# A recurrent kernel's matmuls regrouped: output rows by half of batch and column set, 256 columns an instruction

## The chip, the cores and the metric

The kernel runs on one core of a Trainium2 chip. A core has a matrix engine (TensorE, in the profile PE for its matmuls and PEld for its weight loads), VectorE (DVE), ScalarE (ACT), GpSimd (POOL) and SyncE (SP), whose queue issues most DMAs. SBUF is the working memory of 128 partitions; PSUM, of 8 banks, takes the results of matmuls. The metric is the device time of one execution in microseconds.

## The reference

A GRU over 128 time steps, whose outputs are added to its input. Batch 64, width 512; all in float32.

```
do_prop = ((t + 1) % 4 == 0) & (t < T - 1)
z = sigmoid([x_t, h] @ Wz + bz)
r = sigmoid([x_t, h] @ Wr + br)
c = tanh([x_t, r * h] @ Wh + bh)
h_new = (1 - z) * h + z * c              # the output of step t
h     = tanh(h_new @ Wp + bp) if do_prop else h_new
out[:, t] = x[:, t] + h_new
```

Each of Wz, Wr and Wh is 1024 x 512: the upper half multiplies x_t, which is known for all steps ahead, and the lower half multiplies h, which is not. So a step has three dependent-on-h products (R and Z from h, H from r * h), a fourth (P, with Wp) every fourth step, and products of x that may be done at any time before.

## The kernel before

**Layout.** The 64 batch rows are two halves of V = 32. A tensor such as h, z or the output has partitions 32q to 32q + 31 for column quarter q (J = 128 columns) and, along the free axis, half h and then the 128 columns: tile [128, 2, 128]. VectorE's 32x32 block transpose (`turn`, L223) makes of it hT, whose slices of 32 columns are the stationary operands, with 128 partitions of contraction.

**Matmuls.** `products` (L195) issues four matmuls, one for each quarter q. All have the same 32-column stationary operand; each streams its own quarter of the weights, 128 columns (96 in the x products), and writes PSUM partitions 32q to 32q + 31. `gate` (L206) calls it for two halves, half 0 first through all four contraction pieces, then half 1: 32 matmuls for a gate. A float32 matmul of the code is two recorded matmuls, each with its weight load: the profile shows 64 for a gate.

**The products of x** are formed for four or eight steps together by a scheme of seven products in place of eight, applied twice: `batch` (L438) covers two of the outer seven products, with seven inner products j each into four scratch banks (q, r, a, x). A *unit* (L442) is one inner product of one outer one: 8 matmuls of the code, 16 recorded, of 96 columns. A batch of two has 14 units. When a batch's first four inner products are done, `end_1` reads them out (ScalarE copies of the x and q banks, two VectorE additions), and after all seven `end_2` does (one copy, three additions). GpSimd then adds batches and biases into tiles cp (L509 to L557), and makes the sums of x that the units need as stationary operands (s12r, s34r, s4r, o, s; L289 to L327). `plain` and `plain_last` (L396, L409) do the first and last steps directly with 128-column matmuls.

**Order.** Each engine's program is in the order of the code. A step (L598 on) is: gate R; for each half sigmoid (ScalarE), r * h (VectorE), transpose; `seed`, which copies the x part of the next step's gate from cp into the gate's PSUM bank, so that the next gate's matmuls accumulate onto it; gate Z; two activations over 256 columns, sigmoid of z and sigmoid of -z, and keep = (1 - z) h; places[0] units; gate H; for each half tanh, times z, plus keep, transpose; places[1] units; in every fourth step gate P, tanh and transpose for each half, places[2] units; then GpSimd's work of that step. The numbers of units are in PLACES (L560), by u, the place in a round of eight steps, and in HEAD and TAIL for the first and last steps. `fill` (L372) runs units from a queue and defers their read-outs to `pending`; `read_out` (L379) issues them behind the next gate. A round of eight steps takes 98 units. u = 0 and 4 are the steps with gate P.

**PSUM.** Four banks for gates: r0 (half 0 of R and of P), r1 (half 1 of R, of P and of H), h (half 0 of H), z (Z, both halves); four scratch banks. The activations of R and H write their result in place into PSUM.

The 112 matmuls of zeros at the start (L185) keep TensorE busy while weights load.

Of the kernel before, what the change touches and what calls it, by code (L numbers as in the profile page):

```python
# [12 lines left out]
AF = mybir.ActivationFunctionType  # L13
PSUM = bass.MemoryType.PSUM
# [3 lines left out]
def kernel(  # L18
# [17 lines left out]
    P = 128  # L36
# [11 lines left out]
    assert V * NQ == P and D == H and J == P and T % 8 == 0  # L48

# [54 lines left out]
    bias_in = const.tile([P, 4, J], F32, name="bias")  # L104
# [37 lines left out]
    for q in range(NQ):  # L142
        nc.sync.dma_start(
            out=bias_in[part(q), 3, :],
            in_=bp[ts(q, J)].rearrange("(o n) -> o n", o=1).broadcast_to([V, J]),
        )

    rec = [ps_c.tile([P, 4, J], F32, name=f"rec_{n}") for n in ("r0", "r1", "h", "z")]  # L150
    zz = rec[3][:, :S]
    P_ = 3

    def half(i, h):
        if i == Z:
            return zz[:, h]
        if i == H_:
            return (rec[2][:, 0], rec[1][:, 2])[h]
        return rec[h][:, 0 if i == R else 1]

    scratch = [ps_c.tile([P, 4 * J], F32, name=f"scratch_{n}") for n in "qrax"]
    q_ps, r_ps, a_ps, x_ps = (
# [3 lines left out]
    bias = bias_in.rearrange("p i (c n) -> p c i n", c=C)  # L166

    def spread(bank, rows, which):
        bank = bank.rearrange("p (i n) -> p i n", i=4)
        n = len(which)  # L170
        for q in range(NQ):
            nc.tensor.matmul(
                bank[part(q), 0:n, :],
                lhsT=ones,
                rhs=bias_row[:, rows, ts(q, J)],
                start=True,
                stop=True,
            )
        for j, i in enumerate(which):
            nc.scalar.copy(bias_in[:, i, :], bank[:, j, :])  # L180

    bias0 = bias[:, 0, 0:3, :]
    bias_d = const.tile([P, 3, J // 2], F32, name="bias_d")

    def idle(n):  # L185
        for i in range(n):
            nc.tensor.matmul(
                rec[i // NQ % 4].rearrange("p c n -> p (c n)")[part(i % NQ)],
                lhsT=zeros[:, :V],
                rhs=zeros,  # L190
                start=True,
                stop=True,
            )

    def products(ps, lhs, rhs, start=False):  # L195
        for q in range(NQ):
            nc.tensor.matmul(  # L197
                ps[part(q)],
                lhsT=lhs,
                rhs=rhs(q),  # L200
                start=start,
                stop=True,
                skip_group_check=True,
            )

    def gate(i, lT, w):  # L206
        for h in range(S):
            for k in range(K):
                products(
                    half(i, h), lT[:, h, ts(k, V)], lambda q: w[:, k, ts(q, J)]  # L210
                )

    def product(ps, lT, w, k, start=False):
        c0, s0 = divmod(k, C)
        for h in range(S):
            products(
                ps[:, ts(h, J)],
                lT[:, c0, s0 * B + h * V : s0 * B + (h + 1) * V],
                lambda q: w[:, k, ts(q, J)],
                start and h == 0,  # L220
            )
# [137 lines left out]
    def seed(i, t):  # L359
        if t >= T:  # L360
            return
        src = G[t][:, :, :, i, :].rearrange("p c h n -> p h c n")
        if i == Z:
            nc.scalar.copy(zz.rearrange("p h (c n) -> p h c n", c=C), src)
            return
        for h in range(S):
            nc.scalar.copy(half(i, h).rearrange("p (c n) -> p c n", c=C), src[:, h])  # L367

    queue = []
    pending = []  # L370

    def fill(n):  # L372
        for _ in range(min(n, len(queue))):
            unit, end = queue.pop(0)
            unit()
            if end is not None:
                pending.append(end)

    def read_out():  # L379
        while pending:  # L380
            pending.pop(0)()

    def banks(t):
        first, second = scratch[:2] if t % 2 == 0 else scratch[2:]
        return (first[:, : S * J], first[:, S * J :], second[:, : S * J])

    def add_bias(t, gates):
        new_cp(t // 2)
        for i in gates:
            nc.vector.tensor_add(  # L390
                G[t][:, :, :, i, :],
                banks(t)[i].rearrange("p (h c n) -> p c h n", h=S, c=C),
                bias[:, :, i, :].unsqueeze(2).to_broadcast([P, C, S, J // 2]),
            )
# [43 lines left out]
    def batch(n, ms):  # L438
# [3 lines left out]
        def unit(ps, m, j, e, start):  # L442
            g, i = ms[m]
            a, b = terms(i)[e]
            left, right = lhs(g, a, j), factor(b, j)
            for h in range(S):
                products(
                    ps[:, m, h].rearrange("p (g u) -> p g u", g=3),
                    left[:, ts(h, V)],
                    lambda q: right[:, q],  # L450
                    start and m == 0 and e == 0 and h == 0,
                )
# [11 lines left out]
        def blocks(b, a):  # L464
            return MB[n][:, :nm, b].rearrange("p m h g (a u) -> p m a (h g) u", a=2)[:, :, a]
# [6 lines left out]
        def end_1():  # L472
            MB[n] = mbp.tile([P, 2, 2, S, 3, J // 2], F32, tag="mb", name=f"mb_{what}")
            for m, (g, i) in enumerate(ms):
                M[g, i] = MB[n][:, m]
            T2[n] = copied("cx", "cx", x_ps)
            q1 = copied("cq", "cq", q_ps)
            nc.vector.tensor_add(T2[n][:, :nm], r_ps[:, :nm], T2[n][:, :nm])  # L478
            nc.vector.tensor_add(blocks(0, 0), runs(a_ps[:, :nm]), runs(q1[:, :nm]))

        def end_2():
            q2 = copied("cq", "cq2", q_ps)
            nc.vector.tensor_add(blocks(0, 1), runs(r_ps[:, :nm]), runs(q2[:, :nm]))  # L483
            nc.vector.tensor_add(blocks(1, 0), runs(x_ps[:, :nm]), runs(q2[:, :nm]))
            nc.vector.tensor_add(blocks(1, 1), runs(q_ps[:, :nm]), runs(T2[n][:, :nm]))  # L485

        free = units(a_ps, 2, True)
        one_ = [units(r_ps, 5, True), units(x_ps, 7, True), units(q_ps, 1, True)]

        one_ = sum(one_[2:] + one_[:2] if n in ((1, 0), (1, 1)) else one_, [])  # L490
        two_ = units(x_ps, 4, False) + units(q_ps, 6, False) + units(r_ps, 3, False)
        seq = [(u, None) for u in free + one_ + two_]
        size = sum(len(terms(i)) for _, i in ms)
        for n_units, end in ((4 * size, end_1), (7 * size, end_2)):
            seq[n_units - 1] = (seq[n_units - 1][0], end)
# [19 lines left out]
    def with_bias(g, i, v):  # L515
        m = M[g, i].rearrange("p b h g u -> p (b h) g u")
        nc.gpsimd.tensor_add(m, m, v.unsqueeze(1).to_broadcast([P, 4, 3, J // 2]))  # L517
# [37 lines left out]
    def pair_right(a, p1, x_, g=1):  # L555
        with_bias(g, x_, bias[:, 1, 0:3, :])
        add(c_block(g, a, 1), m_(g, p1), m_(g, x_))  # L557
# [3 lines left out]
        (8, 3, 0), (3, 8, 0), (6, 8, 0), (6, 8, 0), (6, 4, 0), (4, 6, 0), (8, 6, 0), (8, 6, 0),  # L561
    )
    HEAD = {0: (12, 12, 0), 1: (8, 6, 0), 2: (16, 12, 0), 3: (8, 6, 8), 4: (6, 8, 0)}
# [13 lines left out]
    for e in range(3):  # L577
# [4 lines left out]
        if e == H_:  # L582
            read_out()
            for i in range(3):
                seed(i, 0)
        fill(4)
        if e == R:
            spread(scratch[3], slice(0, 2), (R, H_))
            spread(scratch[1], slice(2, 3), (Z,))
            nc.gpsimd.tensor_sub(bias_d, bias[:, 1, 0:3, :], bias0)  # L590
# [3 lines left out]
    read_out()  # L594
# [3 lines left out]
    for t in range(T):  # L598
# [44 lines left out]
        read_out()  # L643
# [14 lines left out]
        rhT = new_T("rhT", f"rhT_{t}")  # L658
        for s_ in range(S):
            r = half(R, s_)  # L660
            nc.scalar.activation(r, r, AF.Sigmoid)  # L661
            nc.vector.tensor_mul(rh[:, s_, :], r, h[:, s_, :])  # L662
# [10 lines left out]
        nc.scalar.activation(z, zz, AF.Sigmoid)  # L673
        nc.scalar.activation(zz, zz, AF.Sigmoid, scale=-1.0)  # L674
        nc.vector.tensor_mul(keep, zz, h)  # L675
# [6 lines left out]
        if prop:  # L682
            for s_ in range(S):
                nc.scalar.copy(half(P_, s_), bias_in[:, 3, :])
        if last:
            nc.gpsimd.tensor_add(xr[g][:, j], xr[g][:, j], keep)
# [13 lines left out]
        read_out()  # L700
        h_new = two.tile([P, S, J], F32, tag="h", name=f"h_{t}")
        hT = None if last else new_T("hT", f"hT_{t}")
        for s_ in range(S):
            c = half(H_, s_)
            nc.scalar.activation(c, c, AF.Tanh)
# [9 lines left out]
            nc.vector.tensor_add(h_new[:, s_, :], c, keep[:, s_, :])  # L715
            turn(hT[:, s_, :], h_new[:, s_, :])
# [8 lines left out]
        if prop:  # L725
            gate(P_, hT, wp)
            read_out()
            h = two.tile([P, S, J], F32, tag="hprop", name=f"hprop_{t}")
            hT = new_T("hT", f"hpT_{t}")
            for s_ in range(S):  # L730
                nc.scalar.activation(h[:, s_, :], half(P_, s_), AF.Tanh)
# [113 lines left out]
```

## Time and profile before

Three runs took 1570.71, 1574.39 and 1577.15 us; the median is 1574.39. The profiled execution took 1573.8 us, its span is 1572.0 us.

| | busy us | share of the span | instructions |
|---|---|---|---|
| TensorE matmuls (PE) | 1369.3 | 87% | 51,920 |
| TensorE weight loads (PEld) | 1261.9 | 80% | 51,920 |
| VectorE (DVE) | 776.7 | 49% | 2,163 |
| ScalarE (ACT) | 561.7 | 36% | 1,858 |
| GpSimd (POOL) | 885.4 | 56% | 1,030 |

The granted clock of TensorE has a mean of 0.986: about three quarters in the first 78 us, 1.00 after that. The span has three parts: the first 78.3 us, in which weights load and step 0 runs; 127 steps of which eight in the middle take 94.5 us (from one GpSimd addition of a round, at 795.49 us, to the same in the next, at 890.03); and 4.8 us from the last matmul (1567.2 us) to the end, in which the last output is written.

How to read it: an idle time stands before an instruction with what ended it, an engine or a DMA; "issue" stands where nothing that the profile shows ended it. Matmuls overlap, so the mean duration of one (273 ns at 128 columns) isn't the distance to the next; rates are read from stretches.

### The profile page before, as it was taken

The numbers are of one execution on the slowest core, as the hardware profiler recorded it, in microseconds if no ns is written. First come the engines' busy times: TensorE is split into PE (matmuls) and PEld (weight loads), VectorE is DVE, ScalarE is ACT, GpSimd is POOL, SyncE is SP. The second block draws the span as 40 slices with busy tenths as digits, with TensorE's granted clock in tenths as the row PEclk, the third lists the DMA queues.
The fourth block names the chain that finished last, engine by engine and source line by source line (L and its number), as shares of the span: only waits on it lengthen the run. The fifth ranks groups of instructions, "written<-read, shape, count | busy, mean of one in ns | idle before, by whom it ended". The sixth has DMA issues, their size and how long they took to land.

```text
span 1572.0 us, 111797 instructions
## 1 busy us (share of the span) xinstructions
PE 1369.3 (87%) x51920; PEld 1261.9 (80%) x51920; DVE 776.7 (49%) x2163; ACT 561.7 (36%) x1858; POOL 885.4 (56%) x1030
## 2 busy tenths in 40 slices
PE   6588888889888888988888888889888988988888
PEld 4578888888788888888888888888778888878887
DVE  0345554554554554554554554554454555555544
ACT  0023333333333333333333333333333433333333
POOL 2276666656565665666656565565656655566520
PEclk7799999999999999999999999999999999999999
DMA  2321110111111111210111111111110111110021
GB/s 99 108 60 44 42 35 21 41 45 45 31 36 39 32 45 31 56 34 20 43 44 45 31 36 39 34 44 32 51 34 22 45 44 45 31 32 25 25 75 47
DMA packets 114221, 66.38 MB, mean 42 GB/s; under 512 B 12604, under 2 KB 108988, under 8 KB 113756
## 3 DMA queue, kind: packets, MB, share of 16 engines
q1 hardware_dynamic: 113048, 58.90, 13.5%
q8 instruction: 407, 6.67, 1.8%
q14 instruction: 58, 0.48, 0.1%
q10 hardware_dynamic: 452, 0.20, 0.0%
q0 software_dynamic: 256, 0.14, 0.0%
HBM read 42.41 MB, written 16.78 MB: 38 GB/s over the span
## 4 chain that ended last, share of the span: by engine, by line
PE 83%; issue 11%; SPq 3%; DMA 2%; POOL 1%; ACT 0%; DVE 0%; POOLq 0%; DVEq 0%; ACTq 0%
PE rec_r L197 27%; PE rec_z L197 15%; PE scratch_x L197 10%; PE scratch_q L197 10%; PE scratch_r L197 10%; PE rec_h L197 7%; PE scratch_a L197 5%; SPq L93 3%; DMA wh<-in_L_cond_Wh_dram 1%; DMA wh<-in_L_cond_Wr_dram 1%; DMA xr<-in_x_dram 0%; POOL cp L513 0%; POOL mb L517 0%; DVE keep L675 0%; ACT z L673 0%
## 5 line engine op out<-in xcount | busy, mean ns | idle before, releaser
L197 PE MATMUL rec_r<-wh,hT 128*32 128x128 f32 x6144 | 206.7, 273 | 32.4 <-issue 31.8
L197 PE MATMUL rec_z<-wh,hT 128*32 128x128 f32 x6144 | 207.7, 273 | 11.5 <-issue 9.9
L197 PEld LDWEIGHTS rec_r<-wh,hT 128*32 128x32 f32 x6144 | 176.7, 110 | 44.3 <-issue 43.2
L197 PEld LDWEIGHTS rec_z<-wh,hT 128*32 128x32 f32 x6144 | 180.3, 110 | 22.7 <-issue 22.1
L782 POOL TENSOR_TENSOR xr<-xr,h 128x256 f32<-128x256 f32 x127 | 92.8, 731 | 168.3 <-DVE h L715 159.6
L513 POOL TENSOR_TENSOR mb<-mb,mb 128x768 f32<-128x768 f32 x58 | 105.9, 1826 | 138.8 <-DVE mb L485 138.8
L197 PE MATMUL rec_h<-wh,rhT 128*32 128x128 f32 x4096 | 156.0, 273 | 21.8 <-issue 18.5
L197 PE MATMUL rec_r<-wh,rhT 128*32 128x128 f32 x4096 | 157.4, 273 | 15.7 <-issue 12.7
L513 POOL TENSOR_TENSOR cp<-mb,mb 128x768 f32<-128x768 f32 x75 | 136.9, 1826 | 48.0 <-DVE mb L485 36.5
L661 ACT ACTIVATE rec_r<-rec_r 128x128 f32<-128x128 f32 x256 | 67.1, 262 | 248.9 <-PE rec_r L197 248.9
L197 PEld LDWEIGHTS rec_h<-wh,rhT 128*32 128x32 f32 x4096 | 123.5, 110 | 31.5 <-issue 26.3
L197 PEld LDWEIGHTS rec_r<-wh,rhT 128*32 128x32 f32 x4096 | 127.0, 110 | 24.0 <-issue 20.1
L367 ACT COPY rec_r<-cp 128x128 f32<-128x128 f32 x384 | 102.7, 268 | 103.7 <-DVE h L715 68.9
L478 DVE TENSOR_TENSOR cx<-scratch_r,cx 128x384 f32<-128x384 f32 (+1 forms) x107 | 59.3, 554 | 158.3 <-ACT cx L469 158.3
L517 POOL TENSOR_TENSOR mb<-mb,bias 128x768 f32<-128x768 f32 x35 | 63.8, 1823 | 128.9 <-DVE mb L485 128.9
L469 ACT COPY cq<-scratch_q 128x384 f32<-128x384 f32 (+1 forms) x214 | 101.5, 474 | 66.0 <-PE scratch_q L197 63.6
L483 DVE TENSOR_TENSOR mb<-scratch_r,cq 128x384 f32<-128x384 f32 (+1 forms) x107 | 59.3, 554 | 119.5 <-PE scratch_r L197 96.0
L675 DVE TENSOR_TENSOR keep<-rec_z,h 128x256 f32<-128x256 f32 x96 | 40.8, 425 | 151.5 <-ACT rec_z L674 151.5
L673 ACT ACTIVATE z<-rec_z 128x256 f32<-128x256 f32 x128 | 49.1, 383 | 139.2 <-PE rec_z L197 139.2
L513 POOL TENSOR_TENSOR cp<-cp,mb 128x768 f32<-128x768 f32 x29 | 52.9, 1823 | 71.6 <-DVE mb L485 70.5
L662 DVE TENSOR_TENSOR rh<-rec_r,h 128x128 f32<-128x128 f32 x192 | 55.6, 290 | 64.5 <-ACT rec_r L661 63.9
L513 POOL TENSOR_TENSOR cp<-mb 128x768 f32<-128x768 f32 x47 | 85.7, 1824 | 2.7 <-ACT rec_r L367 0.2
(150 smaller groups left out, 3320.8 us busy)
## 6 DMA issues: line engine op xcount, KB each, us to landing
out_dram<-xr SPq DMA_DIRECT2D x249, 64.0 KB
xr<-in_x_dram SPq DMA_DIRECT2D x248, 64.0 KB
xs<-in_x_dram SPq DMA_DIRECT2D x240, 64.0 KB
wx<-in_L_cond_Wr_dram SPq DMA_DIRECT2D x7, 256.0 KB
wx<-in_L_cond_Wz_dram SPq DMA_DIRECT2D x7, 256.0 KB
wx<-in_L_cond_Wh_dram SPq DMA_DIRECT2D x7, 256.0 KB
wh<-in_L_cond_Wr_dram SPq DMA_DIRECT2D x4, 256.0 KB
wh<-in_L_cond_Wz_dram SPq DMA_DIRECT2D x4, 256.0 KB
```

The lines of the kernel that those rows point to most:

```text
L93: eng.dma_start(out=wt[:, k, :], in_=w.rearrange("(q k e) n -> k q e n", q=NQ, k=K)[k],)
L197: nc.tensor.matmul(ps[part(q)], lhsT=lhs, rhs=rhs(q), start=start, stop=True, skip_group_check=True,)
L367: nc.scalar.copy(half(i, h).rearrange("p (c n) -> p c n", c=C), src[:, h])
L469: nc.scalar.copy(c[:, :nm], ps[:, :nm])
L478: nc.vector.tensor_add(T2[n][:, :nm], r_ps[:, :nm], T2[n][:, :nm])
L483: nc.vector.tensor_add(blocks(0, 1), runs(r_ps[:, :nm]), runs(q2[:, :nm]))
L513: nc.gpsimd.tensor_add(dst, a, b)
L517: nc.gpsimd.tensor_add(m, m, v.unsqueeze(1).to_broadcast([P, 4, 3, J // 2]))
L661: nc.scalar.activation(r, r, AF.Sigmoid)
L662: nc.vector.tensor_mul(rh[:, s_, :], r, h[:, s_, :])
L673: nc.scalar.activation(z, zz, AF.Sigmoid)
L782: nc.gpsimd.tensor_add(xr[g][:, j], xr[g][:, j], h_new)
```

## The change

- `products` issues its four matmuls for half h of the batch and column set c: PSUM partitions 32(2h + c) on, with the stationary operand of half h, streaming two quarters of the weights, q = c and q = 2 + c, in one matmul of 256 columns (192 in the x products). A gate is 16 matmuls of the code in place of 32, a unit 4 in place of 8. Both halves run through the contraction together.
- So a gate's PSUM rows are by (h, c), and its free axis by d (quarter q = 2d + c). The rest of the kernel keeps the layout by quarter. `crossed` moves between them: each sigmoid or tanh of a half is two instructions on 64 partitions, which read partitions 64h on and write partitions 64d on of an SBUF tile. R, Z, H and P have four activations each (before: 2, 2, 2 and 2).
- r and c are SBUF tiles; the sigmoid of -z is gone, and keep is (z - 1) h from one VectorE instruction, so that h_new = c - keep, done for both halves in one instruction and turned in one.
- `seed` is one copy of 256 columns for every gate; biases are held in the new row order (bias_x, bias_p).
- Gates take three PSUM banks (r with P, z, h), scratch takes five: the x bank has a second one, y, and batches alternate.
- A batch's read-out is split into five parts, each put in the queue where its bank is complete (`end_x`, `end_q`, `end_r`, `end_q2`, `end_r2`), and run at once, with no `pending`. All batches use one order of inner products: a, x, q, r, x, q, r.
- PLACES is new: the units stand elsewhere in the steps, with 98 in a round as before, and 5 of them behind gate P in u = 0 and 4. HEAD differs by two units in step 4.

```diff
+    bias_x = const.tile([P, C, S, 3, J // 2], F32, name="bias_x")
+    bias_p = const.tile([P, S, J], F32, name="bias_p")
...
-    rec = [ps_c.tile([P, 4, J], F32, name=f"rec_{n}") for n in ("r0", "r1", "h", "z")]
-    zz = rec[3][:, :S]
+    rec = [ps_c.tile([P, S, 2, J], F32, name=f"rec_{n}") for n in "rzh"]
     P_ = 3
+    def gate_ps(i):
+        return rec[0][:, 1] if i == P_ else rec[i][:, 0]
+
+    scratch = [ps_c.tile([P, 4 * J], F32, name=f"scratch_{n}") for n in "qraxy"]
...
+    def quarters(v):
+        return v.rearrange("p n (d c j) -> p c n d j", d=2, c=2)
...
     def products(ps, lhs, rhs, start=False):
-        for q in range(NQ):
-            nc.tensor.matmul(
-                ps[part(q)],
-                lhsT=lhs,
-                rhs=rhs(q),
+        for h in range(S):
+            for c in range(2):
+                nc.tensor.matmul(
+                    ps[part(2 * h + c)],
+                    lhsT=lhs(h),
+                    rhs=rhs(c),
...
+    def gate(i, lT, w):
+        for k in range(K):
+            products(
+                gate_ps(i), lambda h: lT[:, h, ts(k, V)], lambda c: quarters(w)[:, c, k]
             )
...
+    def crossed(dst, h, ps, func):
+        for d in range(2):
+            nc.scalar.activation(
+                dst[ts(d, 2 * V), h, :], ps[ts(h, 2 * V), d, :], func
             )
...
     def seed(i, t):
+        if t < T:
+            nc.scalar.copy(
+                gate_ps(i).rearrange("p d (c n) -> p d c n", c=C),
+                G[t][:, :, :, i, :].rearrange("p c d n -> p d c n"),
+            )
...
-            for h in range(S):
-                products(
-                    ps[:, m, h].rearrange("p (g u) -> p g u", g=3),
-                    left[:, ts(h, V)],
-                    lambda q: right[:, q],
-                    start and m == 0 and e == 0 and h == 0,
-                )
+            products(
+                ps[:, m].rearrange("p d (g u) -> p d g u", g=3),
+                lambda h: left[:, ts(h, V)],
+                lambda c: right[:, c::2],
+                start and m == 0 and e == 0,
+            )
...
+        x_ps = x_two[len(T2) % 2]
...
+        for ps, j, start, end in (
+            (a_ps, 2, True, None),
+            (x_ps, 7, True, end_x),
+            (q_ps, 1, True, end_q),
+            (r_ps, 5, True, end_r),
+            (x_ps, 4, False, None),
+            (q_ps, 6, False, end_q2),
+            (r_ps, 3, False, end_r2),
+        ):
...
     PLACES = (
-        (8, 3, 0), (3, 8, 0), (6, 8, 0), (6, 8, 0), (6, 4, 0), (4, 6, 0), (8, 6, 0), (8, 6, 0),
+        (1, 8, 5), (1, 9, 0), (4, 8, 0), (6, 8, 0), (1, 8, 5), (6, 8, 0), (0, 8, 0), (1, 11, 0),
     )
-    HEAD = {0: (12, 12, 0), 1: (8, 6, 0), 2: (16, 12, 0), 3: (8, 6, 8), 4: (6, 8, 0)}
+    HEAD = {0: (12, 12, 0), 1: (8, 6, 0), 2: (16, 12, 0), 3: (8, 6, 8), 4: (6, 10, 0)}
...
+        r = two.tile([P, S, J], F32, tag="r", name=f"r_{t}")
         for s_ in range(S):
-            r = half(R, s_)
-            nc.scalar.activation(r, r, AF.Sigmoid)
-            nc.vector.tensor_mul(rh[:, s_, :], r, h[:, s_, :])
+            crossed(r, s_, gate_ps(R), AF.Sigmoid)
+            nc.vector.tensor_mul(rh[:, s_, :], r[:, s_, :], h[:, s_, :])
             turn(rhT[:, s_, :], rh[:, s_, :])
...
-        nc.scalar.activation(z, zz, AF.Sigmoid)
-        nc.scalar.activation(zz, zz, AF.Sigmoid, scale=-1.0)
-        nc.vector.tensor_mul(keep, zz, h)
+        for s_ in range(S):
+            crossed(z, s_, gate_ps(Z), AF.Sigmoid)
+        nc.vector.scalar_tensor_tensor(
+            out=keep, in0=z, scalar=1.0, in1=h, op0=ALU.subtract, op1=ALU.mult
+        )
...
         for s_ in range(S):
-            c = half(H_, s_)
-            nc.scalar.activation(c, c, AF.Tanh)
+            c = cand[:, s_, :]
+            crossed(cand, s_, gate_ps(H_), AF.Tanh)
             nc.vector.tensor_mul(c, c, z[:, s_, :])
...
-            nc.vector.tensor_add(h_new[:, s_, :], c, keep[:, s_, :])
-            turn(hT[:, s_, :], h_new[:, s_, :])
+        if not last:
+            nc.vector.tensor_sub(h_new, cand, keep)
+            turn(hT, h_new)
```

## The prediction

> **What bounds the kernel now.** I read four views, in this order: the page, the waits of the weight loads, their timeline, and the chain that ended last.
>
> ```profile
> span 1572.0 us, 111797 instructions
> ...
> PE 1369.3 (87%) x51920; PEld 1261.9 (80%) x51920; DVE 776.7 (49%) x2163; ACT 561.7 (36%) x1858; POOL 885.4 (56%) x1030
> ...
> q8 instruction: 407, 6.67, 1.8%
> ...
> PE 83%; issue 11%; SPq 3%; DMA 2%; POOL 1%; ACT 0%; DVE 0%; POOLq 0%; DVEq 0%; ACTq 0%
> ```
>
> TensorE is the bound: no other engine has a share worth naming in the chain. But 11% of that chain is "issue", time in which TensorE waits for nothing that the profile shows. The waits of the weight loads say how much (columns: total us, times, longest us):
>
> ```profile
> PEld rec_r L197 <- issue: 76.3, 99, 1.7
> PEld scratch_q L197 <- issue: 37.8, 55, 1.4
> PEld scratch_r L197 <- issue: 34.9, 54, 1.2
> PEld scratch_x L197 <- issue: 34.0, 50, 1.3
> PEld rec_h L197 <- issue: 26.3, 30, 1.7
> PEld rec_z L197 <- issue: 23.6, 47, 1.0
> PEld scratch_a L197 <- issue: 14.9, 26, 1.0
> ```
>
> That is 247.8 us in 361 holes, spread over all tiles in the same way, so no tile's data is late. The timeline says when they come (start, us, what, and in brackets the idle time before it):
>
> ```profile
> 800.13 1.03 PEld L197 LDWEIGHTS rec_r<-wh,hT 128*32 128x32 f32 x39 [1.53 <-issue]
> ...
> 803.97 0.16 PEld L197 LDWEIGHTS scratch_x<-tt,o 128*32 128x32 f32 x8 [0.52 <-issue]
> ...
> 807.51 0.25 PEld L197 LDWEIGHTS rec_r<-wh,rhT 128*32 128x32 f32 x9 [0.60 <-issue]
> ...
> 811.02 0.22 PEld L197 LDWEIGHTS scratch_q<-wx,o 128*32 128x32 f32 x9 [0.83 <-issue]
> ...
> 814.63 0.25 PEld L197 LDWEIGHTS rec_z<-wh,hT 128*32 128x32 f32 x10 [0.24 <-issue]
> ...
> 818.59 0.25 PEld L197 LDWEIGHTS rec_h<-wh,rhT 128*32 128x32 f32 x9 [1.16 <-issue]
> ...
> 822.36 0.23 PEld L197 LDWEIGHTS scratch_x<-tt,s12r 128*32 128x32 f32 x11 [0.84 <-issue]
> ...
> 825.87 1.13 PEld L197 LDWEIGHTS rec_z<-wh,hT 128*32 128x32 f32 x43 [0.34 <-issue]
> ```
>
> Work resumes after a hole every 3.68 us (25.74 us over 7). The page has 2 x 51920 TensorE instructions and 407 packets on the instruction queue, 16.4 KB each: 255 instructions to a packet, or 128 pairs of weight load and matmul. Counted in the timeline's rows from 90 to 1540 us, 327 of 357 distances between holes hold 120 to 130 matmuls, so the holes stand at packet boundaries. What decides is the period: where fewer than 40 of the 128 belong to gates (the longer ones), the block runs 2.75 us and the hole is 0.98, together 3.73; with 80 to 100 it is 3.20 and 0.49, together 3.69; above 100 it is 3.40 and 0.43, together 3.83. The hole shrinks as the work grows. A fetch of about 3.7 us (3.4 to 4.1 in nine of ten blocks) runs beside the block before it, and whoever is shorter waits.
>
> The rate of the matmuls themselves is in the chain that ended last:
>
> ```profile
> 801.43 1.75 PE rec_z L197 x64
> ...
> 804.34 0.66 PE scratch_q L197 x32
> ```
>
> 64 matmuls of 128 columns take 1.75 us, 32 of 96 columns 0.66. Four of them run side by side in the four row groups of the output: 109.4 ns a four at 128 columns, 82.5 at 96, so 0.84 ns a column and 1.9 ns fixed. Instructions cost nearly nothing inside a block; columns do.
>
> **The sum of before, as a check.** Step 1 starts at 78.3 us (first matmul of its gate R). After it come 127 steps of three gates and 31 of Wp, 412 gates of 64 recorded matmuls: 412 x 1.75 = 721. The 96-column rows add to 24,080 matmuls, 16 to a unit: 1505 units x 0.33 = 497. 24 units of the plain tail at 128 columns: 10.5. With 78.3 that is 1306.5; holes 247.8 and 4.8 us from the last matmul to the end make 1559 of 1572. The 13 us left are short waits.
>
> **The change, part by part.**
>
> *Half the instructions, twice the columns (`products`, `gate`, `product`, `unit`).* A gate becomes 32 recorded matmuls of 256 columns, a unit 8 of 192. A four of 256 columns costs 0.84 x 256 + 1.9 = 217 ns, a gate 8 of these, 1.736 us; a unit 2 of 163.3, 0.327; a plain unit 0.434. Lower bound: half of what four cost before (no column dearer, 1.70 if the fixed part and more vanished); upper bound: twice the 128-column four, 218.8. Both ends lie within 2%. Streaming: 412 x 1.736 + 1505 x 0.327 + 24 x 0.434 = 1218, 10 us less than before.
>
> *The fetch.* About 204 packets in place of 407; 128 pairs now run 128/4 x 163.3 = 5.2 us to 6.9 us, against a fetch of 3.4 to 4.1. The holes go: -247.8 us. The bounds are 0 left and, if the 0.43 us seen in the fullest blocks is a floor paid at each boundary, 204 x 0.43 = 88 left. I take 0, because 28 of 357 distances hold 254 to 383 matmuls: they pass one or two boundaries without a visible hole.
> [...]
>
> *The chains after the gates.* Both batch halves now end together, and each activation is split by 64 partitions. Before, for the second half of R:
>
> ```profile
> 801.54 0.26 ACT L661 ACTIVATE rec_r<-rec_r 128x128 f32<-128x128 f32 x1 [0.67 <-PE rec_r L197]
> ...
> 801.84 0.29 DVE L662 TENSOR_TENSOR rh<-rec_r,h 128x128 f32<-128x128 f32 x1 [0.29 <-ACT rec_r L661]
> ...
> 802.16 0.31 DVE L224 STREAM_TRANSPOSE rhT<-rh 128x128 f32<-128x128 f32 x1
> ```
>
> The next gate's first matmul stood at 801.21; count from it. ScalarE starts at +0.33; no row has a 64-partition activation. Bounds: 0.20 each (half of a back-to-back pair of 128x128 copies, 0.46 for two, so 0.20 start to start), or twice the 0.26 row, 0.52. I take 0.26 with starts 0.20 apart, as the row has the same 128 elements a partition. Half 0 is ready at +0.79, its multiply ends at +1.12, its transpose at +1.46; half 1's multiply at +1.78, transpose at +2.12, TensorE at +2.16 (a transpose's end to the next matmul is 0.03 to 0.04 in the rows). Cover: gate Z, 1.736, and places[0] units of 0.327. With none (u = 6) it misses by 0.42, with one (u = 0, 1, 4, 7) by 0.10, with four or more by nothing. After H: half 1's tanh +1.19, multiply +1.52, a 256-column subtract (row 0.43) +1.98, a 256-column transpose (0.43) +2.44, TensorE +2.48; 8 units cover 2.62. After Wp: +1.58, 5 units cover 1.64. In u = 7 the x bank is used again after four units while its copy stands behind four tanh and a seed on ScalarE: 0.5. Per eight steps 4 x 0.10 + 0.42 + 0.5 = 1.3 us, over 14 rounds 19. In the tail, with 0 and 3 to 5 units: 6 x 0.42 + 4.6 after H + 1.6 after Wp = 8.7. Head steps 1 and 3 (6 units after H): 1.0. The end: 5.5 in place of 4.8.
>
> *What lies beside this at no cost.* ScalarE gains five activations and loses about 0.3 us of seeds a step: 4.4 us a step becomes 5.4 of 9.7. VectorE loses small instructions. GpSimd's queue is the cover most worth watching: 58 us per eight steps, in 94.5 before and 78 after. Walked in order: each x sum is wanted a step or more after its place (o12 and s56 of an odd group end about 0.8 us before step u = 4, wanted 7 us into it), and a step's seeds come 3.8 us or more after the sums they copy. If the cover failed, each late sum would hold TensorE for its lateness. SP's DMAs are not moved; the Wp bias takes four DMAs as before.
>
> **Sum.** 78.3 + 1218 + 19 + 8.7 + 1.0 + 5.5 = 1330.5 span, and 1.8 us around it (1573.8 against 1572.0): 1332. The median shown is 0.6 us above the profiled execution, within its spread.
>
> **Rivals.**
> 1. *A floor at each boundary.* For it: 0.43 us even in blocks above 3.4 us. Against: the 28 distances that pass a boundary without a hole. 1332 + 88 = 1420 at most; half of it, 1376.
> 2. *The split activations are the new bound (slower).* For it: the chains are longer by 0.9 us each and the halves no longer hide one another. At 0.52 each in series, R's chain is +3.12, H's +3.70, Wp's +2.80: waits of about 6.3, 8 and 2.4 us per eight steps, 16.7 in all, 267 over 16 rounds less the 19 counted, so 1580, level with before. Above 0.55 us each the change loses. Against: the row of the same length is 0.26.
> 3. *The holes aren't fetch and stay.* 1574 - 10 + 24 = 1588. Against: the constant period.
>
> **How the numbers follow.** No holes and short chain waits: 0.77, with its own range 1303 (no chain wait) to 1368 (chain waits doubled). A floor: 0.12, 1368 to 1420. Activations at the bound: 0.06, half of it above 1582. Holes stay: 0.05, mostly slower. A measurement tells about 0.5% from no change. Faster 0.91, same 0.02, slower 0.07. The range goes from 1303 up to 1400, half of the second case.
>
> **What would show it.** Right: some 204 instruction packets; "issue" under 2% of the chain; a gate of 32 matmuls in 1.74 us; a round of eight steps in 78 us, not 94.5. Wrong: holes at each 128 pairs still; 64-partition rows well above 0.26 us; waits of rec_h for rhT or of rec_r for hT of a microsecond in all steps; waits of scratch tiles for GpSimd's s or o tiles.

## The result: 1.1% slower, where 15% faster was predicted

The changed kernel takes 1592.8 us (median of 4 runs, 1589.65 to 1594.99). The kernel before takes 1575.77 us beside it (4 runs, 1570.71 to 1580.85). The ratio is 1.0107, with a 95% interval of 1.0069 to 1.0145. The profiled execution took 1592.18 us, its span is 1590.4 us. The prediction was 1332 us.

**The profile after.** The page shows that the instruction stream was halved, as predicted, and that VectorE, which the prediction had at no cost, is busy 980.6 us in place of 776.7 with fewer instructions (1909 in place of 2163):

```profile
span 1590.4 us, 59768 instructions
...
PE 1377.0 (87%) x26024; PEld 923.5 (58%) x26024; DVE 980.6 (62%) x1909; ACT 750.7 (47%) x2401; POOL 910.1 (57%) x1030
...
q8 instruction: 204, 3.34, 0.9%
```

The waits of the weight loads (total us, times, longest us) were 247.8 us of "issue" before. Now two waits for VectorE's transposes head the list:

```profile
PEld rec_r L201 <- DVE hT L232: 129.8, 64, 5.4
PEld rec_h L201 <- DVE rhT L232: 74.9, 90, 1.7
PEld rec_r L201 <- issue: 39.8, 122, 1.9
PEld rec_z L201 <- issue: 28.5, 109, 5.6
PEld rec_h L201 <- ACT rec_r L369: 17.9, 14, 1.3
PEld scratch_x L201 <- ACT cx L468: 13.2, 22, 3.5
PEld scratch_y L201 <- ACT cx L468: 9.7, 21, 0.9
```

rec_r is gate R, which needs hT; rec_h is gate H, which needs rhT. The transposes themselves have kept their length (311 ns against 312 for 128 columns). What stands ahead of them has not. These are the groups of instructions by shape, after (count | busy us, mean ns | idle us before them and what ended it):

```profile
L718 DVE TENSOR_TENSOR c<-c,z 128x128 f32<-128x128 f32 x256 | 148.8, 589 | 144.7 <-ACT c L227 142.8
L673 DVE TENSOR_TENSOR rh<-r,h 128x128 f32<-128x128 f32 x192 | 140.5, 732 | 173.3 <-ACT r L227 173.3
L728 DVE TENSOR_TENSOR h<-c,keep 128x256 f32<-128x256 f32 x127 | 103.2, 813 | 12.4 <-DVE c L718 0.5
L686 DVE SCALAR_TENSOR_TENSOR keep<-z,h 128x256 f32<-128x256 f32 x96 | 78.7, 819 | 55.2 <-ACT z L227 55.2
```

and the same work in the kernel before:

```profile
L662 DVE TENSOR_TENSOR rh<-rec_r,h 128x128 f32<-128x128 f32 x192 | 55.6, 290 | 64.5 <-ACT rec_r L661 63.9
L706 DVE TENSOR_TENSOR rec_h<-rec_h,z 128x128 f32<-128x128 f32 x128 | 37.7, 294 | 23.5 <-ACT rec_h L705 23.1
L715 DVE TENSOR_TENSOR h<-rec_h,keep 128x128 f32<-128x128 f32 x127 | 37.0, 292 | 10.1
L675 DVE TENSOR_TENSOR keep<-rec_z,h 128x256 f32<-128x256 f32 x96 | 40.8, 425 | 151.5 <-ACT rec_z L674 151.5
```

Same engine, same shape (only h is now one instruction of 256 columns in place of two), and the same operation (only keep now subtracts too). The difference is in the names: before, the first operand is rec_r, rec_h or rec_z, a PSUM bank; after, it is r, c or z, an SBUF tile. The mean hides two populations: about 54% of the products still take 0.29 us, the others up to 1.92. GpSimd is as busy in the kernel before: 147 of its 192 products r * h in the row above start while a GpSimd instruction runs, and none of them takes more than 0.294 us. In the changed kernel no product of r * h or c * z that starts without one takes more than 0.295 us. The timeline of one stretch shows what sets the length of a long one (start, us; in brackets the idle time before it):

```profile
805.30 1.91 PE L201 MATMUL rec_r<-wh,hT 128*32 128x256 f32 x32
...
807.03 1.91 PE L201 MATMUL rec_z<-wh,hT 128*32 128x256 f32 x32
...
812.62 0.29 DVE L718 TENSOR_TENSOR c<-c,z 128x128 f32<-128x128 f32 x1
812.64 1.95 POOL L526 TENSOR_TENSOR mb<-mb,mb 128x768 f32<-128x768 f32 x1 [4.04 <-DVE mb L495]
...
813.20 1.54 DVE L718 TENSOR_TENSOR c<-c,z 128x128 f32<-128x128 f32 x1 [0.29 <-ACT c L227]
...
814.55 1.85 POOL L531 TENSOR_TENSOR mb<-mb,bias_d 128x768 f32<-128x768 f32 x1
...
814.85 1.83 DVE L728 TENSOR_TENSOR h<-c,keep 128x256 f32<-128x256 f32 x1
...
816.72 0.45 DVE L232 STREAM_TRANSPOSE hT<-h 128x256 f32<-128x256 f32 x1
...
817.22 3.35 PE L201 MATMUL rec_r<-wh,hT 128*32 128x256 f32 x32 [2.65 <-DVE hT L232]
...
820.39 1.90 PE L201 MATMUL rec_z<-wh,hT 128*32 128x256 f32 x32
```

The first c * z runs before GpSimd's addition and takes 0.29 us. The second starts while GpSimd adds (812.64 to 814.59) and ends at 814.74, 0.15 us after GpSimd. The subtraction starts beside the next addition (which ends at 816.40) and ends at 816.68, 0.28 us after it. Over the whole trace, each slow product of 128 columns ends 0.148 us (median; 0.147 to 0.152 in 8 of 10) after the end of the GpSimd instruction that ran when it started, and each slow one of 256 columns 0.281 us (0.280 to 0.284). Nothing passes between the two engines here: they work on different tiles.

There is a second cost in the same lines. The gate at 805.30 hands over to the next at 807.03: 1.73 us, the price that was predicted. The gate at 817.22, after a hole of 2.65 us, hands over at 820.39: 3.17 us. TensorE ran at half its rate in most of it: the granted clock is 0.54 from 817.20 to 820.40 us, and 1.00 from 805.30 to 807.00. The windows show that in the granted clock (here 800 to 1100 us; the columns are the length, busy us of PE, PEld, DVE, ACT and POOL with counts, then the clock, the DMA share and GB/s), first after, then before:

```profile
800.00:1100.00 300.00, 266.81 (x5144) 183.55 (x5144) 195.39 (x379) 151.17 (x482) 181.61 (x206) 0.97 0.13 36
```

```profile
800.00:1100.00 300.00, 266.02 (x10291) 246.82 (x10294) 153.62 (x428) 112.58 (x372) 178.79 (x210) 1.00 0.14 36
```

213 fours of gate matmuls after 80 us take 0.38 to 0.45 us in place of 0.217, some 45 us in all; 194 of them lie where the clock record has half rate. Most of the "issue" rows of rec_r and rec_z above are these: 0.2 us before the next four.

**Where the miss went.** The span is 1590.4 us in place of the 1330.5 predicted, 260 more. The waits for hT and rhT, the 17.9 us of rec_h for the seed copy, and the 22.9 for the copies cx come to 245.5 us. 29 us were predicted for the chains; 217 are beyond that. With 45 us of half rate that makes 262. So the 248 us of fetch holes did go, and about as much came back, most of it behind VectorE. That GpSimd is the cause is so far only read from the ends of instructions; the runs below test it.

### The profile page after: what moved, and what is told of

It reads as the page before. It is cut to its first block, busy times and chain, and to the rows that moved or that the text cites. A ratio compares the mean times of both kernels' runs of the same rounds, so it can differ in the third digit from the quotient of the medians.

```text
span 1590.4 us, 59768 instructions
## 1 busy us (share of the span) xinstructions
PE 1377.0 (87%) x26024; PEld 923.5 (58%) x26024; DVE 980.6 (62%) x1909; ACT 750.7 (47%) x2401; POOL 910.1 (57%) x1030
## 5 line engine op out<-in xcount | busy, mean ns | idle before, releaser
L227 ACT ACTIVATE r<-rec_r 64x128 f32<-64x128 f32 x512 | 139.3, 272 | 411.8 <-PE rec_r L201 405.6
L201 PE MATMUL rec_h<-wh,rhT 128*32 128x256 f32 x4096 | 283.0, 381 | 53.8 <-DVE rhT L232 50.9
L201 PE MATMUL rec_r<-wh,hT 128*32 128x256 f32 x3072 | 211.5, 422 | 107.7 <-DVE hT L232 106.8
L673 DVE TENSOR_TENSOR rh<-r,h 128x128 f32<-128x128 f32 x192 | 140.5, 732 | 173.3 <-ACT r L227 173.3
L201 PEld LDWEIGHTS rec_h<-wh,rhT 128*32 128x32 f32 x4096 | 144.2, 110 | 163.2 <-DVE rhT L232 74.9
L718 DVE TENSOR_TENSOR c<-c,z 128x128 f32<-128x128 f32 x256 | 148.8, 589 | 144.7 <-ACT c L227 142.8
L227 ACT ACTIVATE c<-rec_h 64x128 f32<-64x128 f32 x512 | 139.2, 272 | 206.6 <-PE rec_h L201 200.4
L201 PE MATMUL rec_z<-wh,hT 128*32 128x256 f32 x3072 | 199.3, 403 | 0.0
L227 ACT ACTIVATE z<-rec_z 64x128 f32<-64x128 f32 x512 | 139.2, 272 | 51.5 <-PE rec_z L201 40.0
L728 DVE TENSOR_TENSOR h<-c,keep 128x256 f32<-128x256 f32 x127 | 103.2, 813 | 12.4 <-DVE c L718 0.5
L232 DVE STREAM_TRANSPOSE rhT<-rh 128x128 f32<-128x128 f32 x256 | 79.7, 311 | 8.9
```

The costliest lines, as they stand in the source:

```text
L201: nc.tensor.matmul(ps[part(2 * h + c)], lhsT=lhs(h), rhs=rhs(c), start=start, stop=True, skip_group_check=True,)
L227: nc.scalar.activation(dst[ts(d, 2 * V), h, :], ps[ts(h, 2 * V), d, :], func)
L232: nc.vector.transpose(out=dst, in_=src)
L673: nc.vector.tensor_mul(rh[:, s_, :], r[:, s_, :], h[:, s_, :])
L718: nc.vector.tensor_mul(c, c, z[:, s_, :])
L728: nc.vector.tensor_sub(h_new, cand, keep)
```

## The experiments

Theory one: the products lost their PSUM operand, and a VectorE instruction with both inputs in SBUF waits for the GpSimd instruction that is running. Its rivals: the activations by 64 partitions, or the three gate banks, make the chains longer; or the time of half the instructions was never to be had. The runs were on three chips; on these the kernel before took 1616.82 us (first four runs), 1597.75 (next four) and 1576.31 (last two). Each run is compared with the kernel before on its own chip.

**1. r and c back to PSUM.** Everything else is the changed kernel: 256-column matmuls, four activations a gate. r and c go to columns of the gate banks that are free at that time. The subtraction and the last transpose are done by half again.

```diff
-        r = two.tile([P, S, J], F32, tag="r", name=f"r_{t}")
+        r = (rec[2][:, 1, 0], rec[0][:, 1, 1])
...
-        cand = two.tile([P, S, J], F32, tag="r", name=f"c_{t}")
+        cand = (rec[1][:, 1, 0], rec[2][:, 1, 1])
...
-            nc.vector.tensor_sub(h_new, cand, keep)
-            turn(hT, h_new)
+            nc.vector.tensor_sub(h_new[:, s_, :], c, keep[:, s_, :])
+            turn(hT[:, s_, :], h_new[:, s_, :])
```

> The changed kernel, with r and the candidate c written to spare PSUM columns (two banks, one for each half) in place of SBUF tiles, so that r * h, c * z and c - keep each have one operand in PSUM again; subtraction and transpose again by half. Theory A (a VectorE instruction with both inputs in SBUF waits for the GpSimd instruction that is running): r * h falls from a mean of 0.73 us to 0.29, c * z from 0.59 to 0.29, the waits of PE and PEld for rhT and hT fall from 205 us to under 30, the granted clock goes back to 0.98, and the time to 1340 to 1390 us. Rival B (the chains are too long in themselves, since both halves end together and each activation is split): durations may fall, but the waits for rhT and hT stay above 100 us and the time above 1500. keep = (z - 1) h still has two SBUF inputs and stays near 0.8 us; it is off the path.

Measured: 1407.23 us, ratio 0.8717 (0.8693 to 0.874), somewhat above the 1340 to 1390 expected. The products have their old length, with the same activations ahead of them; groups by shape:

```profile
L718 DVE TENSOR_TENSOR rec_z<-rec_z,z 128x128 f32<-128x128 f32 x128 | 38.1, 298 | 66.6 <-ACT rec_z L227 66.6
...
L673 DVE TENSOR_TENSOR rh<-rec_h,h 128x128 f32<-128x128 f32 x96 | 27.9, 291 | 111.5 <-ACT rec_h L227 111.5
```

The waits for hT and rhT fell from 204.7 to 43.6 us. The clock record has one stretch at half rate after the first 80 us, of 3.41 us; in the changed kernel it has 25, 92 us in all. keep, (z - 1) h, still has two SBUF inputs and still takes 0.695 us in the mean, but nothing waits for it. What is at the head of the weight loads' waits now is new:

```profile
PEld scratch_x L201 <- ACT cx L468: 36.8, 23, 3.5
PEld scratch_y L201 <- ACT cx L468: 32.3, 21, 2.0
PEld rec_r L201 <- DVE hT L232: 30.1, 74, 0.8
PEld rec_h L201 <- DVE rhT L232: 13.5, 47, 0.5
```

c now stands in the bank of gate H. The seed of that bank, a copy on ScalarE, waits until VectorE has read c for the last time (ScalarE stands idle 139.7 us before these copies until the subtraction ends), and the copies cx stand behind it in ScalarE's queue. Run 7 takes that up.

**2. The other way round: the kernel before, with r and c in SBUF.** Nothing else is changed.

```diff
-            r = half(R, s_)
-            nc.scalar.activation(r, r, AF.Sigmoid)
-            nc.vector.tensor_mul(rh[:, s_, :], r, h[:, s_, :])
+            nc.scalar.activation(r[:, s_, :], half(R, s_), AF.Sigmoid)
+            nc.vector.tensor_mul(rh[:, s_, :], r[:, s_, :], h[:, s_, :])
...
-            c = half(H_, s_)
-            nc.scalar.activation(c, c, AF.Tanh)
+            c = cand[:, s_, :]
+            nc.scalar.activation(c, half(H_, s_), AF.Tanh)
```

> The kernel before, with one thing of the change alone: sigmoid and tanh write r and c to SBUF tiles, so that r * h, c * z and h = c + keep have two SBUF inputs. Matmuls, halves, activations' sizes and order are those of before. Theory A: r * h goes from 0.29 us to 0.5 or more, c * z and h likewise, TensorE gets waits for hT and rhT of 40 us or more, and the time rises to 1600 to 1660 us. Rival B: durations and time stay, 1570 to 1580.

Measured: 1665.56 us, ratio 1.0306 (1.027 to 1.0342). The products are as slow as in the changed kernel, with whole activations of 128 partitions and 128-column matmuls:

```profile
L716 DVE TENSOR_TENSOR h<-c,keep 128x128 f32<-128x128 f32 x254 | 219.5, 864 | 14.4
L707 DVE TENSOR_TENSOR c<-c,z 128x128 f32<-128x128 f32 x256 | 157.7, 616 | 32.8 <-ACT c L706 31.0
L662 DVE TENSOR_TENSOR rh<-r,h 128x128 f32<-128x128 f32 x192 | 124.0, 646 | 30.3 <-ACT r L661 28.8
```

So the place of the operand is enough to make them slow. How that reaches TensorE was expected otherwise: the weight loads' waits that name hT come to 14.2 us and none names rhT, where 40 or more were expected, while 29.2 us end with ScalarE's r and the issue rows grow from 247.8 to 278.6. It costs 49 us here and some 185 in the changed kernel. That the fetch holes of the old one give its chains time is the likely reason (run 4 shows such cover), but it was not tested here.

**3. GpSimd's additions in thirds.** The changed kernel; each addition of 768 columns is three of 256. Nothing on VectorE, ScalarE or TensorE is edited.

```diff
-        nc.gpsimd.tensor_add(dst, a, b)
+        for n in range(3):
+            nc.gpsimd.tensor_add(dst[:, ts(n, 2 * J)], a[:, ts(n, 2 * J)], b[:, ts(n, 2 * J)])
```

> The changed kernel, with each GpSimd addition of 768 columns (1.83 us) cut into three of 256 (0.73 each by the row of the xr addition). Theory A in its strict form (VectorE waits until the running GpSimd instruction is over): the longest wait falls from 1.8 to 0.73 us and the mean excess of r * h from 0.44 to about 0.2, so the waits for rhT and hT at least halve and the time falls to 1430 to 1530 us, though GpSimd's own busy time grows by some 20%. If the two share bandwidth instead, VectorE's rows stay as they are in the mean and the time stays at 1580 to 1600. Rival B: no change.

Measured: 1436.53 us, ratio 0.8897 (0.8873 to 0.8921). GpSimd is busy longer (997.1 us in place of 910.1), and VectorE's products are shorter:

```profile
L723 DVE TENSOR_TENSOR c<-c,z 128x128 f32<-128x128 f32 x256 | 127.6, 515 | 128.0 <-ACT c L227 126.3
L678 DVE TENSOR_TENSOR rh<-r,h 128x128 f32<-128x128 f32 x192 | 85.9, 447 | 147.9 <-ACT r L227 147.9
...
L733 DVE TENSOR_TENSOR h<-c,keep 128x256 f32<-128x256 f32 x127 | 74.9, 589 | 12.4 <-DVE c L723 0.5
```

The wait is for one GpSimd instruction, not for GpSimd's work: shorter instructions let VectorE in between them, and 99 of 100 products c * z take at most 0.82 us (before the edit, 1.90). hT's waits fall to 63.8 us, rhT's to 24.2.

**4. The instructions doubled again, on top of run 1.** Each matmul of 256 (192) columns is two of half the columns.

```diff
-        for h in range(S):
-            for c in range(2):
-                nc.tensor.matmul(
-                    ps[part(2 * h + c)],
...
-                    rhs=rhs(c),
+        for d in range(2):
+            for h in range(S):
+                for c in range(2):
+                    nc.tensor.matmul(
+                        ps[part(2 * h + c), d],
...
+                        rhs=rhs(c)[:, d],
```

> The first experiment's kernel, with each matmul of 256 (192) columns issued as two of 128 (96) over the four row groups, so the instructions double and nothing else changes. If the holes of the kernel before are instruction fetch, they come back: 407 packets, a block of 128 matmuls every 3.7 us, issue holes of 200 us or more, and 1560 to 1610 us. If they are not, the time is that of the first experiment plus 10 us of fixed cost.

Measured: 1611.06 us, 204 us more than run 1 on the same chip; ratio to before 0.9971 (0.9945 to 0.9997). There are 406 instruction packets again, and the holes that end by "issue" are back in all tiles, 244.6 us in all. In this kernel as in the one before, a hole ends 1.39 us after an instruction packet has landed (median of 324 and 355 holes; 1.23 to 1.58 us in 9 of 10):

```profile
PEld rec_r L202 <- issue: 53.8, 61, 1.6
PEld scratch_r L202 <- issue: 43.4, 51, 1.4
PEld rec_z L202 <- issue: 37.2, 55, 5.4
```

The period between holes is again the same whatever the block holds: blocks with few gate matmuls (under 40 of the 128) run 2.83 us and wait 0.97, those with many (80 or more) run 3.35 and wait 0.48, 3.8 us in both. The holes of 244.6 us cost only 204, probably since chains hide in them: the waits for hT and rhT are 3.9 and 3.8 us here, and those for cx 36.8 in place of 69.1. This is the gain that the prediction had in its sum, shown by itself.

**5. The changed kernel once more, on the second chip,** unedited.

> The changed kernel as it is, on the chip of the following three, so that they can be set against it. On the chip of the first four experiments the kernel before took 1617 us where it took 1576 beside the change; if that difference is the fetch of instructions, the changed kernel, which has no fetch holes, takes the same 1585 to 1600 us here whatever the kernel before takes.

Measured: 1593.03 us, the 1592.8 of the first measurement again. But the kernel before takes 1597.75 us on this chip, so the ratio is 0.9968 (0.9952 to 0.9984). The same change is 1.1% slower on one chip and 0.3% faster on another. What varies is the kernel that is bound by the fetch: between 1576 and 1617 us on the three chips. The mean distance between instruction packets (of those below 5 us) was 3.74 us in the profile of the kernel before, and 3.87 and 3.82 in runs 2 and 4 on the chip where it takes 1617; 0.1 us over 407 packets is 41 us. That the fetch makes the difference between the chips is worked out from these, not shown by itself.

**6. GpSimd's additions shortened.** The changed kernel with the same number of GpSimd instructions; each addition of 768 columns is done on 48 of them. It leaves out the rest of each sum, so it computes something else than the reference.

```diff
-        nc.gpsimd.tensor_add(dst, a, b)
+        nc.gpsimd.tensor_add(dst[:, :48], a[:, :48], b[:, :48])
...
-        nc.gpsimd.tensor_add(m, m, v.unsqueeze(1).to_broadcast([P, 2, 3 * J]))
+        nc.gpsimd.tensor_add(
+            m[:, :, :24], m[:, :, :24], v[:, :24].unsqueeze(1).to_broadcast([P, 2, 24])
+        )
```

> The changed kernel, with GpSimd's additions of 768 columns done for their first 48 columns alone (cp in two tiles that are zeroed once); 15/16 of these additions are left out, all the rest stands, with the operands in SBUF. Theory A: what GpSimd still runs is 0.73 us for xr and 0.3 to 0.7 for the sums of x, so r * h, c * z and h come to within 0.1 us of their free durations in the mean, the waits for hT and rhT fall below 60 us and the time to 1340 to 1390 us. If operands in PSUM had another merit than missing GpSimd, the time stays above 1450.

Measured: 1383.66 us, ratio 0.8665 (0.8644 to 0.8686), 209 us less than the changed kernel on the same chip. The products' means are 0.352 us for r * h and 0.369 for c * z, with both inputs still in SBUF: the operands' place costs little when GpSimd's instructions are short. The waits for hT and rhT are 36.1 and 14.4 us. With runs 1 and 2 this closes the loop: two SBUF inputs and a long GpSimd instruction are both needed.

**7. The seed of gate H later, on top of run 1.** The copy onto the bank in which c stands is issued behind the step's second group of units.

```diff
-        if t < T - 2:
-            seed(H_, t + 1)
...
+        if t < T - 2:
+            seed(H_, t + 1)
```

> The first experiment's kernel (r and c in PSUM), with the seed of the next gate H issued behind the units that follow gate H, not ahead of them. There the seed waits on ScalarE for VectorE to be done with c in the same bank, and the copies of the x banks stand behind it: 69 us of waits of the x and y scratch banks for these copies. If that order is their cause they fall below 15 us and the time from 1407 to 1345 to 1365 us. If the copies are late for another reason (four tanh and VectorE's chain alone), the time stays above 1390.

Measured: 1358.78 us, ratio 0.8512 (0.8491 to 0.8532). The waits for cx are 10.6 us in place of 69.1. TensorE is busy 97% of the span, and its weight loads wait for:

```profile
PEld rec_r L201 <- DVE hT L232: 39.9, 98, 0.8
PEld rec_h L201 <- DVE rhT L232: 16.9, 61, 0.5
PEld scratch_x L201 <- ACT cx L468: 7.0, 8, 3.5
```

Eight steps in the middle take 79.4 us; 78 was predicted for the changed kernel, which takes 95.4 (the same GpSimd addition at 853.96 and 949.36 us). 98 waits of 0.4 us are left after H, where eight units don't cover the chain.

**8. Runs 7 and 3 together.** With r and c in PSUM, are GpSimd's long additions still a cost?

```diff
-        nc.gpsimd.tensor_add(dst, a, b)
+        for n in range(3):
+            nc.gpsimd.tensor_add(dst[:, ts(n, 2 * J)], a[:, ts(n, 2 * J)], b[:, ts(n, 2 * J)])
```

> The kernel of the run before this one, with GpSimd's additions in thirds as well. What is left of two SBUF inputs, keep = (z - 1) h, waits less (0.63 us in the mean in the first experiment, 0.42 free), but it isn't on the path and GpSimd is busy some 100 us longer. Theory A: within 10 us of the run before this one. If keep's wait is on the path by way of VectorE's order, 10 to 30 us faster.

Measured: 1357.28 us, ratio 0.8502 (0.8483 to 0.8522). The same as run 7 (1358.78) to 0.1%, with the same waits (40.4 for hT, 17.0 for rhT). What thirds won in run 3 they don't win here.

**9. r alone in PSUM.** The changed kernel, with only r moved back; c, and so the last subtraction, stay in SBUF.

```diff
-        r = two.tile([P, S, J], F32, tag="r", name=f"r_{t}")
+        r = (rec[2][:, 1, 0], rec[0][:, 1, 1])
```

> The changed kernel with r alone in PSUM; c and h = c - keep keep their two SBUF inputs. It splits the loss between the two chains. In the profile of the changed kernel the weight loads wait 75 us for rhT and 130 us for hT, and 45 us go to matmuls at half clock behind long holes. Theory A: the waits for rhT fall below 20 us, those for hT and the half clock stay, and the time is 1490 to 1530 us. If r's chain were the whole of it, the time would be near 1407; if it were nothing, near 1593.

Measured: 1525.51 us, ratio 0.9672 (0.9641 to 0.9703), some 67 us less than the changed kernel. The waits for rhT fall from 74.9 to 5.8 us, while those for hT grow from 129.8 to 153.0. So the larger part of the loss is in the chain after H, with two products and a subtraction in series that can each wait for GpSimd.

**10. Run 7 with the units placed anew,** one more of them behind H in most steps, to cover the 0.4 us left.

```diff
-        (1, 8, 5), (1, 9, 0), (4, 8, 0), (6, 8, 0), (1, 8, 5), (6, 8, 0), (0, 8, 0), (1, 11, 0),
+        (1, 9, 4), (1, 9, 0), (3, 9, 0), (5, 9, 0), (1, 9, 4), (5, 9, 0), (0, 8, 0), (2, 10, 0),
```

> The kernel with r and c in PSUM and the later seed (1359 us), with one unit moved behind gate H in five of the eight steps, since its weight loads still wait 0.40 us for hT behind eight units: PLACES (1,9,4), (1,9,0), (3,9,0), (5,9,0), (1,9,4), (5,9,0), (0,8,0), (2,10,0), 98 in all. Each of five waits for hT should shrink by 0.33 us and two for hpT grow by as much: 3 x 0.33 x 15 rounds, some 10 to 18 us, so 1341 to 1352. If the waits aren't made by the cover, 1359 stays.

Measured: 1408.84 us, ratio 0.8931 (0.8908 to 0.8955): 50 us more than run 7, on another chip. The waits for hT did fall, to 13.3 us. But a batch now ends at another place in the step, and its read-out stands in VectorE's queue behind the chain of gate H; the units of the next batch wait for the bank:

```profile
PEld scratch_r L201 <- DVE mb L494: 51.4, 43, 1.5
PEld rec_r L201 <- DVE hT L232: 13.3, 27, 0.9
```

Smaller waits came too: 11.6 us for VectorE's addition into cx (3.1 in run 7), 12.3 for the tanh behind gate P, which lost a unit of cover (3.4), and 12.3 for GpSimd's sums s (none). A unit's place covers a chain and also decides behind what the read-out of its batch is queued. The first was counted when this run was planned, the second was not.

## Why the prediction was wrong, step by step

- **Half the instructions, twice the columns: right.** A gate of 32 recorded matmuls takes 1.73 us (805.30 to 807.03), 1.736 was predicted, where the clock is full.
- **The fetch: right.** 204 packets, no holes at 128 pairs, and run 4 brings 244.6 us of them back by doubling the instructions. No floor is left at each boundary (rival 1): in run 7 all "issue" rows come to 19 us. Rival 3 ("the holes aren't fetch and stay", 1588) has nearly the number measured, and its mechanism is false: the holes went, and other waits of the same size came. A time that agrees says nothing on a cause.
- **The activations by 64 partitions: right in length, not in spacing.** 0.272 us each against the estimate of 0.26, and run 1 keeps all of them at 1407 us. Rival 2, which needs 0.52 each, is false:

```profile
L227 ACT ACTIVATE r<-rec_r 64x128 f32<-64x128 f32 x512 | 139.3, 272 | 411.8 <-PE rec_r L201 405.6
```

  But "starts 0.20 apart" was taken from a pair of copies. The timeline of the changed kernel has four in 1.14 us, 0.29 from start to start, where the prediction's chains have 0.86; each chain is 0.28 us longer by that alone:

```profile
812.03 1.14 ACT L227 ACTIVATE c<-rec_h 64x128 f32<-64x128 f32 x4 [0.99 <-PE rec_h L201]
```

- **The chains after the gates: the step that failed.** "Half 0 is ready at +0.79, its multiply ends at +1.12" takes 0.29 us for the multiply and "(row 0.43)" for the subtraction. Both come from rows of instructions that read PSUM: the names in the fence, rec_r, stood beside the number. The change makes both inputs SBUF tiles, and the rows measured 0.732, 0.589 and 0.813 us in the mean, up to 1.97. No row of the trace before had an r, c or z product with two SBUF inputs, so this price was one to bound from both sides, and it was taken as known.
- **"What lies beside this at no cost": failed for the same reason.** "VectorE loses small instructions" counts instructions; their time grew by 204 us. "GpSimd's queue is the cover most worth watching" looked at GpSimd's results being late. They weren't: its tiles hold TensorE for 1.3 us in all. What came was that GpSimd's instructions, 58 us in eight steps and 33 of them in additions of 768 columns, hold up VectorE instructions of other tiles. Runs 1, 2, 3 and 6 agree, and in the changed kernel's trace the slow ones end 0.148 us (128 columns) and 0.281 us (256) after GpSimd's instruction. The prediction had no term for such a wait.
- **Not in the sum at all: the clock.** Waits were priced at their own length. Behind 25 of the 33 holes above 2 us the matmuls also ran at half rate for 3.41 or 6.83 us, which cost about 45 us in all.
- **The range** went to 1400, on the ground of boundaries and activations alone. With r and c in PSUM and the seed moved, the kernel takes 1358.78 us, 2% above the 1332. Most of that difference is in the waits for hT and rhT, 56.8 us in run 7 where 29 were predicted for all chains; the spacing of the activations is a part of them, and the rest wasn't taken apart. So the plan of half the instructions was sound. Of the 260 us missed, the operands' place cost some 185 (run 1), and the order of the seed, once r and c were back in PSUM, another 48 (run 7).
- **Smaller slips, on which nothing hangs.** Chain waits doubled make 1361, not 1368. Rival 2's waits, from its own chain ends and covers, come to 15.4 us per eight steps, not 16.7. ScalarE gains six activations a step, not five, and is busy 1.5 us a step longer, not 1.0.

## What to carry to other kernels

When a change moves an operand from PSUM to SBUF, take no duration from the row before: look for a GpSimd instruction that runs beside it, and add up to that instruction's length to each VectorE instruction that then has two SBUF inputs (here up to 1.6 us beside additions of 1.83 us), above all where several stand in series ahead of a matmul. If there is one, leave one operand in PSUM, or cut the GpSimd instructions short (here 1407 us in run 1 and 1437 in run 3, in place of 1593). And if you take instructions away from a fetch-bound TensorE, work out anew which waits the holes used to hide: here those for hT and rhT were 7.7 us in run 4, with holes, and 43.6 in run 1, without.

## What the runs showed of the hardware that was not expected

- VectorE was held up by GpSimd, with which these instructions share no data, for as long as 1.6 us an instruction. In the changed kernel the four kinds of VectorE instruction lose 269 us against their free lengths (0.29 and 0.425 us): 100 in r * h, 77 in c * z, 49 in the subtraction, 43 in keep. GpSimd loses nearly nothing (groups of additions of 768 columns have means of 1.82 to 1.89 us, and 1.82 to 1.83 before).
- The granted clock fell to 0.97 through the middle of the kernel, where it was 1.00 before. Between the first 80 us and the last matmul its record has 25 stretches at half rate, each of 3.41 or 6.83 us. Each follows one hole in TensorE's matmuls of 2.39 to 5.04 us, of which 2.08 us or more lie in the 3.41 us just ahead of the stretch. Where the clock stayed full, no window of 3.41 us on the same grid was idle for more than 2.05 us. 8 holes of 2.61 to 3.77 us had no stretch behind them: a hole's length alone didn't decide, and in this trace a window that was idle for 2.08 us of its 3.41 was enough.
- The kernel before, which is bound by the fetch of instructions, differed by 2.6% between three chips (1576 to 1617 us); the changed kernel, which is bound by chains of engines, did not between two (1592.8 and 1593.0).
